# Mixer gates as 2x2 block products with seven multiplications, mixing in a fixed order, skip on ACT

## The chip, the cores and the metric

The kernel runs on one NeuronCore of a Trainium2 chip. The metric is device time in microseconds, from the start of the program on the chip to its end; lower is better. A core has a matmul engine (PE), a vector engine (DVE), a scalar engine for table functions (ACT), a general engine (POOL) and a queue that here only issues DMAs (SP). Each engine runs its own instructions in order; semaphores tie them together. All data is fp32.

## The reference

A small perceiver layer on x of 8 sequences x 64 tokens x 512 channels: cross attention to a long context, then a state space mixer, then a routed low-rank layer, each added to x. Only the mixer is touched. Per token, with 64 heads in 8 groups:

```
proj = hidden @ in_proj_w.T
gate = proj[..., :I];  hbc = proj[..., I:I + CONV_DIM];  dt = proj[..., -H:]
xBC  = silu(conv(hbc))                  # causal, 4 taps
y    = scan(xBC, softplus(dt), A) + x * D
y    = y / rms(y, per group) * norm_weight * silu(gate)
out  = y @ out_proj_w.T
```

## The kernel before

The mixer (`mixer_and_routed`) holds 512 tokens as four tiles of 128 (`tt`) and works group by group (`g` of 8). `xnT` is the normalized x, transposed: 4 blocks of 128 channels (`dc`) by 512 tokens. A group's input weights `G.w` are ten blocks of 128 output channels: four for the gates (n = 0 to 3), four for x (4 to 7), one each for B and C (8, 9).

- `project(G, n)`, L1101: four matmuls (one per `dc`) of 128x128 by 512 tokens into one PSUM bank of tag "pj", of which there are three. For a gate ACT applies SiLU to the bank (L1111, tile `sg`). For the others DVE runs the four taps (L1116, three times L1122, tile `acc`) and ACT the SiLU (L1127, tile `xbc`).
- `skip`, L1129: y = xbc times D, on POOL (L1134). `load_out`, L995: loads `w_out` and multiplies it by the norm's weight, on POOL (L1004).
- `steps` (POOL, tile `av`, four buffers) and `decay` (PE into two "seg" banks, L1093; ACT Exp, L1098) give a group's decay factors `dec`.
- `mix(G, tt)`, L1136: `pg` (PE), `gm` and `m` (DVE), `px` (PE transposes, L1154), `dx` (DVE). `scan(G, tt)`, L1165: 16 small matmuls `py`, then two DVE adds into `y` (L1178). `gate`, L1191: squares on ACT and POOL, and y times `sg` on DVE (L1194).
- `norm`, L1196: PE sums `pss` (L1200), ACT Ln and Exp (L1203, L1204). `project_out(G, tt)`, L1210: four matmuls into a bank of "pj", then DVE adds to x (L1217).

The groups are pipelined. In one round of the loop (L1275) group G is projected, the old group G-1 is mixed, scanned and gated between those projections, the decays of the new group G+1 follow, then the norm of the old one, then the four gates of G in turn with the four output projections of the old group. ACT needs one table for SiLU and another for Ln and Exp, so its work is kept in blocks by `tc.issue_after(ins)`: every instruction traced in such a block on the engine of `ins` is placed behind `ins` in that engine's queue (order only, no wait for it to finish). Beyond this a planner fixes each engine's order before the run: of the instructions that its own model of time takes to be ready, the one traced earliest goes first, and a tile's buffer is handed out when its first user is placed. The attention's projections already use block products with seven multiplications, by these two tables (L38):

```
FIRST = (("a", "L11", "R11"), ("d", "S2", "T2"), ("b", "S1", "T1"), ("c", "S3", "T3"))
SECOND = (("a", "L12", "R21"), ("b", "S4", "R22"), ("c", "L22", "T4"))
```

L are weight blocks, R token blocks, S sums of weight blocks (`weight_sums`, L137, four POOL adds), T differences of token blocks. The sums a and b lie in one PSUM bank, c and d in another. In the query stage (L209 to L235) `first` of a pair of heads is followed by `second` of the pair before, so one pair's sums are read while another's are computed.

Of the kernel before, what the change touches and what calls it, by code (L numbers as in the profile page):

```python
# [9 lines left out]
F32 = mybir.dt.float32  # L10
# [5 lines left out]
P = 128  # L16
# [934 lines left out]
def mixer_and_routed(ctx, tc, c, x, done, w_in, w_out, w_ra, b_w, out):  # L951
# [43 lines left out]
    def load_out(G):  # L995

        g = G.g
        G.wo = wst.tile([P, GC, D], F32, tag="w_out", name=f"w_out_{g}")
        nc.sync.dma_start(
            out=G.wo, in_=w_out[g * GC * P : (g + 1) * GC * P, :].rearrange("(n p) o -> p n o", p=P)  # L1000
        )
        for n in range(GC):
            ct = g * GC + n
            nc.gpsimd.tensor_scalar(G.wo[:, n, :], G.wo[:, n, :], c.nw[:, ct : ct + 1], None, op0=ALU.mult)  # L1004

    load_in(groups[0])

# [2 lines left out]
    for tt in range(NTT):  # L1010
# [9 lines left out]
            )  # L1020

    dt = big.tile([P, NTT, H2], F32, name="dt")
    z = big.tile([P, NTT, H2], F32, name="sp_z")
    nc.vector.tensor_tensor(z, pdt, c.dtb.unsqueeze(1).to_broadcast([P, NTT, H2]), ALU.add)
    e = big.tile([P, NTT, H2], F32, name="sp_e")

    nc.vector.tensor_scalar(dt, z, 0.0, None, op0=ALU.max)
    nc.vector.scalar_tensor_tensor(out=e, in0=dt, scalar=-2.0, in1=z, op0=ALU.mult, op1=ALU.add)
    nc.scalar.activation(e, e, AF.Exp)
    u = big.tile([P, NTT, H2], F32, name="sp_u")  # L1030
    nc.vector.tensor_scalar(u, e, 1.0, None, op0=ALU.add)
    lu = big.tile([P, NTT, H2], F32, name="sp_lu")
    nc.scalar.activation(lu, u, AF.Ln)
    nc.vector.tensor_scalar(u, u, 1.0, None, op0=ALU.subtract)
    nc.vector.tensor_scalar(z, u, 0.0, None, op0=ALU.is_equal)
# [10 lines left out]
        out=a, in0=dt, scalar=-1.0, in1=a_sb.unsqueeze(1).to_broadcast([P, NTT, H2]),  # L1046
        op0=ALU.mult, op1=ALU.mult,
    )

# [22 lines left out]
    def steps(G, tt):  # L1072


        if tt == 0:
            G.av, G.dec = [], grpp.tile([P, NTT, HPG, S], F32, tag="dec", name="dec")
        av = wk.tile([P, 2, HH, S], F32, tag="av", name="av", bufs=4)
        nc.gpsimd.tensor_tensor(
            av,
            ah[:, :, tt, G.g, :].unsqueeze(3).to_broadcast([P, 2, HH, S]),  # L1080
            c.upto1.unsqueeze(1).unsqueeze(1).to_broadcast([P, 2, HH, S]),
            ALU.mult,
        )
        G.av.append(av)
# [16 lines left out]
    def project(G, n):  # L1101

        pj = bank("pj", [P, NT], "pj", 3)
        for dc in range(DC):
            nc.tensor.matmul(  # L1105
                pj, lhsT=G.w[:, dc, n, :], rhs=xnT[:, dc, :], start=dc == 0, stop=dc == DC - 1
            )
        if n < GC:
            if n == 0:
                G.sg = grpp.tile([P, GC, NT], F32, tag="sg", name="sg")  # L1110
            return nc.scalar.activation(G.sg[:, n, :], pj, AF.Silu).ins  # L1111
        if n == 8:
            G.xbc = grpp.tile([P, GC + 2, NT], F32, tag="xbc", name="xbc")
        ct = G.g * GC + n - GC if n < 8 else (I2 // P + G.g if n == 8 else I2 // P + G2 + G.g)
        acc = wk.tile([P, NT], F32, tag="acc", name="acc", bufs=3)
        nc.vector.tensor_scalar(  # L1116
            acc, pj, c.cw[:, ct, KC - 1 : KC], c.cb[:, ct : ct + 1], op0=ALU.mult, op1=ALU.add
        )
        accb = acc.rearrange("p (b t) -> p b t", b=B)
        pjb = pj.rearrange("p (b t) -> p b t", b=B)  # L1120
        for k in range(1, KC):
            nc.vector.scalar_tensor_tensor(  # L1122
                out=accb[:, :, k:], in0=pjb[:, :, : S - k],
                scalar=c.cw[:, ct, KC - 1 - k : KC - k], in1=accb[:, :, k:],
                op0=ALU.mult, op1=ALU.add,
            )
        return nc.scalar.activation(G.xbc[:, n - GC, :], acc, AF.Silu).ins  # L1127

    def skip(G):  # L1129

        G.y = grpp.tile([P, GC, NT], F32, tag="y", name="y")
        for n in range(GC):
            ct = G.g * GC + n
            nc.gpsimd.tensor_scalar(G.y[:, n, :], G.xbc[:, n, :], c.dk[:, ct : ct + 1], None, op0=ALU.mult)  # L1134

    def mix(G, tt):  # L1136

# [72 lines left out]
    def project_out(G, tt):  # L1210
        po = bank("pj", [P, D], "mo", 3)
        for n in range(GC):
            nc.tensor.matmul(  # L1213
                po, lhsT=G.y[:, n, tt * P : (tt + 1) * P], rhs=G.wo[:, n, :],
                start=n == 0, stop=n == GC - 1,
            )
        nc.vector.scalar_tensor_tensor(  # L1217
            out=x[:, tt, :], in0=po, scalar=G.rs[tt], in1=x[:, tt, :], op0=ALU.mult, op1=ALU.add
        )


    w = big.tile([P, DC, E + E * R], F32, name="w_ra")
# [9 lines left out]
        nc.sync.dma_start(out=bw, in_=b_w)  # L1232

    def route(tt):
        xnT = wk.tile([P, DC, P], F32, tag="xnT", name="rt_xnT")
        layernorm_T(nc, c, small, ps, x, tt, xnT, tag="px", bufs=2, pbufs=1, copy=nc.scalar.copy)
        ph = bank("seg", [P, E + E * R], "ph", 2)
        for dc in range(DC):
            nc.tensor.matmul(
                ph, lhsT=xnT[:, dc, :], rhs=w[:, dc, :], start=dc == 0, stop=dc == DC - 1  # L1240
            )
        top = small.tile([P, 1], F32, tag="top", name="top")
        nc.vector.tensor_reduce(top, ph[:, :E], axis=AX.X, op=ALU.max)
        rw = small.tile([P, E], F32, tag="rw", name="rw")
        nc.vector.scalar_tensor_tensor(
            out=rw, in0=ph[:, :E], scalar=top, in1=rank, op0=ALU.is_equal, op1=ALU.mult
        )
# [12 lines left out]
        whT = wk.tile([P, P], F32, tag="whT", name="whT")  # L1260
        nc.scalar.copy(whT, pt)
        po = bank("y1", [P, D], "ro")
        nc.tensor.matmul(po, lhsT=whT, rhs=bw, start=True, stop=True)
        o = wk.tile([P, D], F32, tag="o", name="o")
        nc.vector.tensor_tensor(o, x[:, tt, :], po, ALU.add)
        nc.sync.dma_start(out=out[tt * P : (tt + 1) * P, :], in_=o)

# [1 line left out]
    g0 = groups[0]  # L1269
    for tt in range(NTT):  # L1270
        steps(g0, tt)
    last = None
    for tt in range(NTT):
        last = decay(g0, tt)
    for g in range(G2):  # L1275
# [10 lines left out]
        with tc.issue_after(last):  # L1286

            for n, behind in (
                (None, ((mix, 0),)),
                (8, ((mix, 1),)),  # L1290
                (9, ((scan, 0),)),
                (4, ((mix, 2), (scan, 1))),
                (5, ((gate, 0), (mix, 3), (scan, 2))),
                (6, ((gate, 1), (scan, 3))),
                (7, ((gate, 2), (gate, 3))),
            ):
                if n is not None:
                    silus.append(project(G, n))
                if old:
                    for what, tt in behind:  # L1300
                        what(old, tt)
            skip(G)
        with tc.issue_after(silus[-1]):
            table = load_ln_exp(nc).ins
        with tc.issue_after(table):
            if new:
                decay(new, 0)
                decay(new, 1)
        gates = [lambda n=n: project(G, n) for n in range(GC)]
        if new:  # L1310
            with tc.issue_after(table):
                last2 = decay(new, 2)
# [1 line left out]
        if old:  # L1314
            with tc.issue_after(table):
                last = norm(old, range(NTT))
        with tc.issue_after(last):
            for n in range(GC):
                if not new and n == NTT - 1:
                    scan(G, n)  # L1320
                    squares(G, n)
                last_gate = gates[n]()
                if not new:

                    for tt in ((0, 1), (2,), (3,), ())[n]:
                        mix(G, tt)
                    if 0 < n < NTT - 1:
                        scan(G, n - 1)
                        squares(G, n - 1)
                    if n == 2:  # L1330
                        scan(G, n)
                        squares(G, n)
                if old:
                    project_out(old, n)
        last = last_gate

    G = groups[-1]
# [77 lines left out]
```

## Time and profile before

| what | us |
|---|---|
| median of 3 runs | 2827.65 (2827.54 to 2829.23) |
| profiled execution, its own time | 2826.02 |
| span of its instructions | 2824.3 |
| one steady period of the mixer, 2400.35 to 2459.73 | 59.38 |
| PE busy in that period | 59.17 |
| DVE busy in that period | 31.13 |
| ACT, POOL busy in that period | 14.25, 23.20 |

The mixer's matmuls run from about 2324 us to the end; attention is before that. In the page's rows a group of instructions is named by line, engine, operation and tiles; a row of the timeline has start, duration, engine, line, operation, tiles, count and, in brackets, how long the engine stood idle before and what ended that. "seg", "pj" and "mo" are PSUM tiles; "mo" is the output projection and shares the "pj" banks. A few groups of the mixer (the columns after the count are busy us and mean ns of one, then idle before it):

```profile
L1105 PE MATMUL pj<-mx_xnT,w_in 128*128 128x512 f32 x640 | 296.3, 603 | 1.3 <-DVE acc L1122 1.3
L1134 POOL TENSOR_SCALAR y<-xbc,small_consts 128x512 f32<-128x512 f32 x32 | 55.7, 1740 | 50.1 <-ACT xbc L1127 50.1
L1004 POOL TENSOR_SCALAR w_out<-w_out,small_consts 128x512 f32<-128x512 f32 x32 | 49.6, 1567 | 179.3 <-DMA w_out<-in_w_out 176.7 <-DMA spare<-in_wo 2.6
L1111 ACT ACTIVATE sg<-pj 128x512 f32<-128x512 f32 x32 | 18.2, 596 | 86.9 <-PE pj L1105 86.8
```

A matmul's duration includes its passage through the pipeline, so the pace of PE is read from the starts. One projection (four matmuls) appears as eight records, 640 in all for 8 groups of 10 blocks.

### The profile page before, as it was taken

The numbers are of one execution on the slowest core, as the hardware profiler recorded it, in microseconds if no ns is written. First come the engines' busy times: TensorE is split into PE (matmuls) and PEld (weight loads), VectorE is DVE, ScalarE is ACT, GpSimd is POOL, SyncE is SP. The second block draws the span as 40 slices with busy tenths as digits, with TensorE's granted clock in tenths as the row PEclk, the third lists the DMA queues.
The fourth block names the chain that finished last, engine by engine and source line by source line (L and its number), as shares of the span: only waits on it lengthen the run. The fifth ranks groups of instructions, "written<-read, shape, count | busy, mean of one in ns | idle before, by whom it ended". The sixth has DMA issues, their size and how long they took to land.

```text
span 2824.3 us, 38454 instructions
## 1 busy us (share of the span) xinstructions
PE 2788.6 (99%) x14972; PEld 1980.9 (70%) x14972; DVE 1745.4 (62%) x3059; ACT 726.6 (26%) x1314; POOL 833.9 (30%) x786
## 2 busy tenths in 40 slices
PE   9899999999999999999999999999999999999998
PEld 7677777777777777777777777777777554444444
DVE  4556676676667666665666676667665416444555
ACT  3322223222222222232222222222222103222222
POOL 4323223222222332223222222322232223433431
PEclk9999999999999999999999999999999999999999
DMA  4822232232113122312311131122212441112200
GB/s 164 276 78 57 76 74 53 53 94 53 46 46 97 46 54 79 74 48 58 94 50 50 46 95 47 46 83 76 48 46 72 146 160 38 53 53 78 79 16 15
DMA packets 277230, 206.02 MB, mean 73 GB/s; under 512 B 155676, under 2 KB 240538, under 8 KB 276026
## 3 DMA queue, kind: packets, MB, share of 16 engines
q1 hardware_dynamic: 277050, 203.57, 25.2%
q8 instruction: 119, 1.95, 0.3%
q14 instruction: 61, 0.50, 0.1%
HBM read 180.87 MB, written 22.66 MB: 72 GB/s over the span
## 4 chain that ended last, share of the span: by engine, by line
PE 83%; DVE 6%; DMA 2%; ACT 1%; issue 0%; POOL 0%; SPq 0%; ACTq 0%; DVEq 0%
PE pav L596 12%; PE psc L526 11%; PE pj L1105 8%; PE pv_a L445 6%; PE pv_b L445 6%; PE pv_c L445 5%; PE pk_a L385 5%; PE pk_b L385 5%; PE pk_c L385 5%; PE mo L1213 4%; PE pv_d L445 3%; PE pk_d L385 2%; PE psn L414 2%; DMA nbs<-max_d 2%; DVE attn L574 1%; PE pvl L468 1%
## 5 line engine op out<-in xcount | busy, mean ns | idle before, releaser
L531 DVE SCALAR_TENSOR_TENSOR attn<-psc,rk,mask_sb 128x256 f32<-128x256 f32 (+1 forms) x832 | 363.4, 473 | 190.5 <-PE psc L526 188.1
L580 POOL TENSOR_TENSOR sm<-attn 128x512 f32<-128x512 f32 x64 | 82.0, 1281 | 1147.6 <-ACT attn L578 1147.6
L596 PE MATMUL pav<-attn,v 128*128 128x256 f32 (+1 forms) x1664 | 384.3, 381 | 0.0
L526 PE MATMUL psc<-q,kT 128*128 128x256 f32 x1536 | 371.5, 381 | 0.0
L596 PEld LDWEIGHTS pav<-attn,v 128*128 128x128 f32 (+1 forms) x1664 | 311.1, 190 | 55.4 <-issue 9.6
L583 POOL TENSOR_TENSOR sm<-sm,attn 128x512 f32<-128x512 f32 x256 | 339.8, 1328 | 29.4 <-DVE attn L574 10.6
L526 PEld LDWEIGHTS psc<-q,kT 128*128 128x128 f32 x1536 | 286.3, 190 | 82.4 <-issue 36.0
L1105 PE MATMUL pj<-mx_xnT,w_in 128*128 128x512 f32 x640 | 296.3, 603 | 1.3 <-DVE acc L1122 1.3
L574 DVE TENSOR_TENSOR attn<-attn,nb 128x1024 f32<-128x1024 f32 x192 | 224.7, 1216 | 68.2 <-ACT nb L571 67.9
L445 PEld LDWEIGHTS pv_a<-wv,cx 128*128 128x128 f32 x1536 | 195.5, 191 | 48.2 <-issue 41.4
L578 ACT ACTIVATE attn<-attn 128x1024 f32<-128x1024 f32 x192 | 202.5, 1058 | 71.3 <-DVE attn L574 68.5
L445 PE MATMUL pv_a<-wv,cx 128*128 128x128 f32 x1536 | 212.7, 279 | 0.0
L542 DVE TENSOR_TENSOR mx<-mx,attn 128x512 f32<-128x512 f32 x256 | 209.5, 818 | 2.0
L1105 PEld LDWEIGHTS pj<-mx_xnT,w_in 128*128 128x128 f32 x640 | 115.2, 190 | 129.4 <-issue 124.7
L385 PE MATMUL pk_a<-cx,wk 128*128 128x417 f32 (+1 forms) x512 | 193.3, 500 | 0.8 <-ACT qrs L110 0.8
L396 ACT ACTIVATE ksq<-kT 128x834 f32<-128x834 f32 (+1 forms) x128 | 109.0, 871 | 159.1 <-DVE kT L377 159.1
L637 POOL TENSOR_TENSOR o<-o,f 128x512 f32<-128x512 f32 x31 | 39.4, 1272 | 306.7 <-DMA f<-sums_d 206.3
L385 PEld LDWEIGHTS pk_a<-cx,wk 128*128 128x128 f32 x512 | 97.2, 190 | 46.1 <-issue 20.8
L1217 DVE SCALAR_TENSOR_TENSOR x<-mo,rs,x 128x512 f32<-128x512 f32 x32 | 24.0, 751 | 165.1 <-PE mo L1213 110.4
L1213 PE MATMUL mo<-w_out,y 128*128 128x512 f32 x256 | 118.1, 597 | 0.0
L571 ACT COPY nb<-nbs 128x256 f32<-128x256 f32 x64 | 24.1, 376 | 324.4 <-DMA nbs<-max_d 324.4
L1122 DVE SCALAR_TENSOR_TENSOR acc<-pj,small_consts,acc 128x504 f32<-128x504 f32 (+1 forms) x144 | 103.9, 725 | 0.7
(220 smaller groups left out, 4230.8 us busy)
## 6 DMA issues: line engine op xcount, KB each, us to landing
wk<-in_wk SPq DMA_DIRECT2D x32, 512.0 KB
wv<-in_wv SPq DMA_DIRECT2D x32, 512.0 KB
w_in<-in_w_in SPq DMA_DIRECT2D x16, 1024.0 KB
wvs<-wv_s_d SPq DMA_DIRECT2D x28, 512.0 KB
wks<-wk_s_d SPq DMA_DIRECT2D x28, 512.0 KB
cx<-in_ctxT SPq DMA_DIRECT2D x16, 834.0 KB
cx<-in_ctxT SPq DMA_DIRECT2D x16, 768.0 KB
wq<-in_wq SPq DMA_DIRECT2D x16, 512.0 KB
```

The costliest lines, as they stand in the source:

```text
L385: nc.tensor.matmul(ps[:, :w], lhsT=u.wk[l][:, dc, :], rhs=u.cx.r[ch][r][:, dc, :], start=start and dc == 0, stop=dc == 1, skip_group_check ...
L396: nc.scalar.activation(sq[ch][:, :, half, :w], u.kT[:, :, half, lo:hi], AF.Square)
L445: nc.tensor.matmul(ps[:, i * HD : (i + 1) * HD], lhsT=u.cx.r[ch][r][:, dc, i * P : (i + 1) * P], rhs=u.wv[l][:, dc, :], start=start and i ...
L526: nc.tensor.matmul(ps[:rows, t - t2, :], lhsT=lhsT, rhs=qh, start=True, stop=True)
L531: nc.vector.scalar_tensor_tensor(out=s.at[:rows, t, :].rearrange("p (h q) -> p h q", h=GQ), in0=ps[:rows, t - t2, :].rearrange("p (h q) -> ...
L542: nc.vector.tensor_tensor(s.mx2, s.mx2, s.at[:, t2 : t2 + 2, :], ALU.max)
L574: nc.vector.tensor_tensor(at[:, k : k + 4, :], at[:, k : k + 4, :], nb.unsqueeze(1).to_broadcast([P, 4, 256]), ALU.add,)
L578: nc.scalar.activation(at[:, k : k + 4, :], at[:, k : k + 4, :], AF.Exp)
L583: nc.gpsimd.tensor_tensor(sm2, sm2, at[:, i : i + 2, :], ALU.add)
L596: nc.tensor.matmul(s.av[:, 0, :], lhsT=u.v[:rows, t, hh, :], rhs=s.at[:rows, t, :], start=t == 0, stop=t == NKT - 1,)
L1105: nc.tensor.matmul(pj, lhsT=G.w[:, dc, n, :], rhs=xnT[:, dc, :], start=dc == 0, stop=dc == DC - 1)
L1213: nc.tensor.matmul(po, lhsT=G.y[:, n, tt * P : (tt + 1) * P], rhs=G.wo[:, n, :], start=n == 0, stop=n == GC - 1,)
```

## The change

The four gate blocks of a group become two 2x2 block products over two halves of the channels and two halves of the tokens (256 each), with seven multiplications each, into two "pj" banks. Token differences are made once, weight sums per group. `skip` and the weighing of `w_out` go from POOL to ACT. Mix and scan are placed on PE behind the projection that they follow in the list, and in the gates' stage the order on PE is fixed: first, second, two output projections, first, second, two output projections. To make room in SBUF some tiles share buffers.

```diff
-        for n in range(GC):
-            ct = g * GC + n
-            nc.gpsimd.tensor_scalar(G.wo[:, n, :], G.wo[:, n, :], c.nw[:, ct : ct + 1], None, op0=ALU.mult)
+    def weigh_out(G):
         for n in range(GC):
+            ct = G.g * GC + n
+            nc.scalar.activation(G.wo[:, n, :], G.wo[:, n, :], AF.Copy, scale=c.nw[:, ct : ct + 1])
+    def sums_in(G, n):
+        l = {
+            f"L{k + 1}{e + 1}": G.w[:, 2 * e : 2 * e + 2, n + k, :] for k in range(2) for e in range(2)
+        }
+        G.l = getattr(G, "l", {})
+        G.l[n] = weight_sums(nc, l, wk.tile([P, 4, 2, P], F32, tag="ws", name="ws"))
...
+    sp = grpp.tile([P, GC, NT], F32, tag="y", name="sp")
...
+    ts = big.tile([P, 4, 2, HT], F32, name="mx_xs")
+    blocks.update((f"T{k + 1}", ts[:, k]) for k in range(4))
+    def token_sums():
+        for o, p, q in (
+            ("T1", "R12", "R11"), ("T2", "R22", "T1"), ("T3", "R22", "R12"), ("T4", "R21", "T2")
+        ):
+            nc.vector.tensor_tensor(blocks[o], blocks[p], blocks[q], ALU.subtract)
...
-        av = wk.tile([P, 2, HH, S], F32, tag="av", name="av", bufs=4)
+        av = wk.tile([P, 2, HH, S], F32, tag="av", name="av", bufs=3)
...
+    def project_gates(G, n):
+        st, l = Group(), G.l[n]
...
+        def first():
+            st.ps = {}
+            for pair in ("ab", "cd"):
+                t = bank("pj", [P, 2, HT], f"pj_{pair}", 3)
+                st.ps[pair[0]], st.ps[pair[1]] = t[:, 0, :], t[:, 1, :]
+            for k, lhs, rhs in FIRST:
+                last = product(k, lhs, rhs, k in "ad", False)
+            p1 = wk.tile([P, HT], F32, tag="p1", name="p1", bufs=1)
+            nc.scalar.copy(p1, st.ps["a"])
+            st.u2 = wk.tile([P, HT], F32, tag="u2", name="u2", bufs=1)
+            nc.vector.tensor_tensor(st.u2, p1, st.ps["d"], ALU.add)
+            nc.vector.tensor_tensor(p1, st.u2, st.ps["b"], ALU.add)
+            nc.vector.tensor_tensor(to[:, 1, HT:], p1, st.ps["c"], ALU.add)
+            return last
+        def second():
+            for k, lhs, rhs in SECOND:
+                last = product(k, lhs, rhs, False, True)
+            nc.scalar.activation(to[:, 0, :HT], st.ps["a"], AF.Silu)
+            nc.vector.tensor_tensor(to[:, 0, HT:], st.u2, st.ps["b"], ALU.add)
+            nc.vector.tensor_tensor(to[:, 1, :HT], st.u2, st.ps["c"], ALU.add)
+            nc.scalar.activation(to[:, 0, HT:], to[:, 0, HT:], AF.Silu)
+            return last, nc.scalar.activation(to[:, 1, :], to[:, 1, :], AF.Silu).ins
...
-            nc.gpsimd.tensor_scalar(G.y[:, n, :], G.xbc[:, n, :], c.dk[:, ct : ct + 1], None, op0=ALU.mult)
+            nc.scalar.activation(G.y[:, n, :], G.xbc[:, n, :], AF.Copy, scale=c.dk[:, ct : ct + 1])
...
-                    silus.append(project(G, n))
+                    done, silu = project(G, n)
+                    silus.append(silu)
                 if old:
-                    for what, tt in behind:
-                        what(old, tt)
+                    with tc.issue_after(done if n is not None else done_out):
+                        for what, tt in behind:
+                            what(old, tt)
             skip(G)
+        if g == 0:
+            token_sums()
+            sums_in(G, 0)
+            sums_in(G, 2)
...
         with tc.issue_after(last):
-            for n in range(GC):
...
+            for k in range(2):
+                first, second = project_gates(G, 2 * k)
+                if k:
+                    own((scan, 3), (squares, 3))
+                    with tc.issue_after(done_out):
+                        done_in = first()
+                else:
+                    done_in = first()
+                    own((mix, 0), (mix, 1))
+                with tc.issue_after(done_in):
+                    done_out, last_gate = second()
+                if not k:
+                    own((scan, 0), (squares, 0))
+                for tt in (2 * k, 2 * k + 1):
+                    if old:
+                        with tc.issue_after(done_out):
+                            done_out = project_out(old, tt)
+                    if not k:
+                        own((mix, tt + 2), (scan, tt + 1), (squares, tt + 1))
+                if new:
+                    sums_in(new, 2 * k)
+            weigh_out(G)
```

`own` runs its steps on G itself in the last round only, where there is no new group. The routed tail takes its `xnT` from the buffers of `sq` and its output tile from those of `acc`.

More of the change, by code (lines that the diff above doesn't have):

```diff
@@ L1022, in mixer_and_routed @@
     dt = big.tile([P, NTT, H2], F32, name="dt")
-    z = big.tile([P, NTT, H2], F32, name="sp_z")
+    sp = grpp.tile([P, GC, NT], F32, tag="y", name="sp")
+    z, e, u, lu = (
+        sp[:, k, : NTT * H2].rearrange("p (t h) -> p t h", h=H2) for k in range(4)
+    )
     nc.vector.tensor_tensor(z, pdt, c.dtb.unsqueeze(1).to_broadcast([P, NTT, H2]), ALU.add)
-    e = big.tile([P, NTT, H2], F32, name="sp_e")
     nc.vector.tensor_scalar(dt, z, 0.0, None, op0=ALU.max)
@@ L1029, in mixer_and_routed @@
     nc.scalar.activation(e, e, AF.Exp)
-    u = big.tile([P, NTT, H2], F32, name="sp_u")
     nc.vector.tensor_scalar(u, e, 1.0, None, op0=ALU.add)
-    lu = big.tile([P, NTT, H2], F32, name="sp_lu")
     nc.scalar.activation(lu, u, AF.Ln)
@@ L1048, in mixer_and_routed @@
     )
+    HT = NT // 2
+    blocks = {
+        f"R{e + 1}{half + 1}": xnT[:, 2 * e : 2 * e + 2, half * HT : (half + 1) * HT]
+        for e in range(2) for half in range(2)
+    }
+    ts = big.tile([P, 4, 2, HT], F32, name="mx_xs")
[5 more added lines that the diff above has]
+            nc.vector.tensor_tensor(blocks[o], blocks[p], blocks[q], ALU.subtract)
     psw = bank("seg", [P, NTT, H2], "psw", 2)
@@ L1104, in project @@
         for dc in range(DC):
-            nc.tensor.matmul(
+            done = nc.tensor.matmul(
                 pj, lhsT=G.w[:, dc, n, :], rhs=xnT[:, dc, :], start=dc == 0, stop=dc == DC - 1
[L1107 to L1111, printed above, removed]
+            ).ins
         if n == 8:
@@ L1126, in project, with product @@
             )
-        return nc.scalar.activation(G.xbc[:, n - GC, :], acc, AF.Silu).ins
+        return done, nc.scalar.activation(G.xbc[:, n - GC, :], acc, AF.Silu).ins
+    def project_gates(G, n):
+        st, l = Group(), G.l[n]
+        if n == 0:
+            G.sg = grpp.tile([P, GC, NT], F32, tag="sg", name="sg")
+        to = G.sg[:, n : n + 2]
+        def product(k, lhs, rhs, start, stop):
+            for dc in range(2):
+                last = nc.tensor.matmul(
+                    st.ps[k], lhsT=l[lhs][:, dc, :], rhs=blocks[rhs][:, dc, :],
+                    start=start and dc == 0, stop=stop and dc == 1, skip_group_check=True,
+                ).ins
+            return last
[12 more added lines that the diff above has]
+            nc.vector.tensor_tensor(to[:, 1, HT:], p1, st.ps["c"], ALU.add)
+            return last
+        def second():
[6 more added lines that the diff above has]
+            return last, nc.scalar.activation(to[:, 1, :], to[:, 1, :], AF.Silu).ins
+        return first, second
     def skip(G):
@@ L1212, in project_out @@
         for n in range(GC):
-            nc.tensor.matmul(
+            last = nc.tensor.matmul(
                 po, lhsT=G.y[:, n, tt * P : (tt + 1) * P], rhs=G.wo[:, n, :],
@@ L1219, in project_out @@
         )
+        return last.ins
     w = big.tile([P, DC, E + E * R], F32, name="w_ra")
@@ L1234, in route @@
     def route(tt):
-        xnT = wk.tile([P, DC, P], F32, tag="xnT", name="rt_xnT")
+        xnT = wk.tile([P, DC, P], F32, tag="sq", name="rt_xnT")
         layernorm_T(nc, c, small, ps, x, tt, xnT, tag="px", bufs=2, pbufs=1, copy=nc.scalar.copy)
@@ L1263, in route @@
         nc.tensor.matmul(po, lhsT=whT, rhs=bw, start=True, stop=True)
-        o = wk.tile([P, D], F32, tag="o", name="o")
+        o = wk.tile([P, D], F32, tag="acc", name="o", bufs=3)
         nc.vector.tensor_tensor(o, x[:, tt, :], po, ALU.add)
@@ L1271, in mixer_and_routed @@
         steps(g0, tt)
-    last = None
+    last = done_out = None
     for tt in range(NTT):
@@ L1308, in mixer_and_routed @@
                 decay(new, 1)
-        gates = [lambda n=n: project(G, n) for n in range(GC)]
         if new:
@@ L1316, in mixer_and_routed, with own @@
                 last = norm(old, range(NTT))
+        def own(*what):
+            if not new:
+                for step, tt in what:
+                    step(G, tt)
         with tc.issue_after(last):
-            for n in range(GC):
[L1319 to L1334, printed above, removed]
+            for k in range(2):
[20 more added lines that the diff above has]
+            weigh_out(G)
         last = last_gate
```

## The prediction

> **What bounds the kernel now.** I read the page's busy times first, then the chain of waits, then the mixer stage alone, because the change touches nothing before 2300 us.
>
> ```profile
> span 2824.3 us, 38454 instructions
> PE 2788.6 (99%) x14972; PEld 1980.9 (70%) x14972; DVE 1745.4 (62%) x3059; ACT 726.6 (26%) x1314; POOL 833.9 (30%) x786
> PE 83%; DVE 6%; DMA 2%; ACT 1%; issue 0%; POOL 0%; SPq 0%; ACTq 0%; DVEq 0%
> ```
>
> PE is the bound: 99% busy, 83% of the chain. The mixer repeats every 59.4 us: the product of y and the gate that the chain passes starts at 2400.35, 2459.73, 2518.99, 2578.39. One period, cut where its character changes, by a view of busy time per stretch:
>
> ```profile
> core 0: us, PE busy (x) PEld busy (x) DVE busy (x) ACT busy (x) POOL busy (x), PEclk, DMA share, GB/s
> 2431.46:2463.40 31.94, 31.94 (x227) 15.37 (x227) 28.88 (x49) 5.67 (x9) 18.50 (x16) 1.00 0.28 96
> 2463.40:2472.40 9.00, 8.79 (x46) 3.86 (x45) 0.00 (x0) 5.02 (x12) 4.69 (x4) 1.00 0.01 2
> 2472.40:2490.90 18.50, 18.50 (x47) 7.93 (x46) 2.27 (x4) 3.56 (x5) 0.00 (x0) 1.00 0.12 36
> ```
>
> Stretch A (first row) runs from the first mix of the old group to the end of the last convolution: DVE has 28.88 of 31.94 us, so it is nearly a bound itself. B (second row) is a chain on ACT. C (third row) is PE alone: gates and output projections. PE is full in all three, in B only because there is unrelated work for it:
>
> ```profile
> 2463.40 0.63 ACT L1127 ACTIVATE xbc<-acc 128x512 f32<-128x512 f32 x1 [3.73 <-DVE acc L1122]
> 2464.05 1.28 ACT L116 ACT_TABLE_LOAD   x1
> 2465.34 0.66 ACT L1098 ACTIVATE dec<-seg 128x256 f32<-128x256 f32 x2
> 2466.75 0.66 ACT L1098 ACTIVATE dec<-seg 128x256 f32<-128x256 f32 x2 [0.75 <-PE seg L1093]
> ...
> 2470.06 0.66 ACT L1098 ACTIVATE dec<-seg 128x256 f32<-128x256 f32 x2 [0.99 <-PE seg L1093]
> 2471.89 0.26 ACT L1203 ACTIVATE rs<-pss,eps 128x4 f32<-128x4 f32 x1 [1.17 <-PE pss L1200]
> 2472.18 0.20 ACT L1204 ACTIVATE rs<-rs 128x4 f32<-128x4 f32 x1
> 2472.40 1.28 ACT L1111 ACT_TABLE_LOAD   x1
> ```
>
> Last SiLU, table load, four decays that alternate with PE, the norm's Ln and Exp. Project 7 ends on PE at 2458.6 (its start 2455.16 plus 3.43). From there to the Exp's end are 13.8 us, in which PE's own share of the chain is four seg blocks of 0.6 and pss 0.95, about 3.4 us. The other 10.3 us are filled by exactly three projections of 3.43 us: gate 0, output projection 0 and gate 1. Three is the number of "pj" banks.
>
> **Part 1: fewer multiplications.** The pace of eight 128x512 matmuls, from the chain in order of time, and of 128x256 ones, from the query stage, where the same seven products run:
>
> ```profile
> 2417.73 3.43 PE pj L1105 x8
> 2421.16 3.43 PE mo L1213 x8
> ```
>
> ```profile
> 103.64 1.03 PE L204 MATMUL pq_cd<-xs,wqs 128*128 128x256 f32 x4
> 103.84 0.37 ACT L220 COPY q_p<-pq_ab 128x256 f32<-128x256 f32 x1 [1.02 <-PE pq_ab L204]
> ...
> 104.50 1.03 PE L204 MATMUL pq_ab<-xnT,wq 128*128 128x256 f32 x4
> 104.77 0.42 DVE L222 TENSOR_TENSOR q_u<-q_p,pq_cd 128x256 f32<-128x256 f32 x1 [3.10 <-PE pq_cd L204]
> ...
> 105.23 0.42 DVE L224 TENSOR_TENSOR q_t<-q_u,pq_ab 128x256 f32<-128x256 f32 x1
> ```
>
> 3.43/8 = 0.429 us against (104.50-103.64)/4 = 0.215 us. Each fp32 matmul is two instructions here (a projection's 4 are 8 records). Gates before: 4x8x0.429 = 13.73 us a group. After: two block products of 7x2x2 = 28 records, 56x0.2155 = 12.07. Gain 1.66 us a group, 13.3 in eight. The Trainium skill speaks against this: "TensorE: Matmul & The Clock Gate", section Back-to-back issue gap, gives sustained 131 ns at 512 columns and 81 ns at 128, so about 98 at 256 by my interpolation; 56x98 = 5.5 us against 32x131 = 4.2 would make the blocks 1.3 times dearer (+4 us a group on our 13.73). The trace halves cleanly at 256 columns, so the row decides.
>
> **Part 2: the new wait, the crux.** The second half of a block product accumulates onto banks that the first half's evacuation must have read. Two things delay that. (a) p1 is an ACT copy traced behind `last`, the norm's Exp: it cannot issue before the end of B. (b) Sums a and b share a bank, so do c and d. The query rows show what this does: the copy of a starts at 103.84, after b's matmuls have ended, although a ended 1.7 us earlier; u2 waits for c; and the read of b ends at 105.65, 1.15 us after the last matmul of the first half issued out (104.50). There another pair's second half fills the hole; here second follows first directly. So `second` of pair 0 starts after Exp + copy 0.4 + u2 0.5 + sum 0.5 = 1.4 us more, and `second` of pair 1 has a hole of 1.25 us. And the output projections, which may go between in the old code, now stand behind `second` (issue_after(done_out)): of the three fillers of B one is left, `first` of pair 0, 3.45 us. PE would lack 6.9 us there.
>
> **What can fill it.** Mixing of the next round is barred too. Projections 8 and 9 of the next group carry no edge on PE; w_in has landed (DMA burst at 2431-2445). Does this program's order reach across groups? It did once:
>
> ```profile
> 2353.97 0.33 PE L1154 MATMUL px<-ident,xbc 128*128 128x128 f32 x1
> 2355.59 0.70 PE L1105 MATMUL pj<-mx_xnT,w_in 128*128 128x512 f32 x1 [1.29 <-DVE acc L1122]
> ```
>
> That transpose belongs to the next round and stands before group 0's gates. So I take it that project 8 (3.43), then mix 1 behind it (0.9), go into B on the third bank, and project 9 starts once that bank's convolution (0.81 + 3x0.73 = 3.0 us) is done.
>
> **Part 3: off POOL, onto ACT and DVE.** POOL loses 4x1.74 (skip) and 4x1.57 (w_out) and gains 8 weight sums at 0.78 (the query rows L141 to L144, 0.75 to 0.82) = 6.2 us; it has slack either way. ACT gains 8 copies of 128x512 at 0.63 (row L1127) and about 1 us in the gates. Only skip 3 matters: it is ready with the last SiLU and traced before the table load, +0.63 us in B; if ordered behind, 0. Should Copy need a table, each change costs 1.28 us; the skill ("ScalarE: Activation LUTs", Table sets) says copy is in every set, which no row here shows. I take 0. DVE gains 10 adds of 0.42 a group in C, where it had 2.27 us of work in 18.5: hidden. Without POOL's skip beside them, gate products may fall from 0.89 to 0.68 us: 0 to -0.8 in A, kept for the range. The four token sums (1.2 us each in the query stage) fall once into DVE's idle 6.4 us before 2350.78; uncovered they cost 4.7. av with three buffers waits for seg 0, 3 segs ahead of its use: 0. Shared tiles in the softplus and the routed tail: used once, at times far apart: 0, at worst 1 us. load_in's DMAs are let go earlier (w_in is done before the last two output projections): 0. The fixed order of mix and scan is the order that PE already shows between 2431 and 2455: 0.
>
> **Sum for a steady group.** A: DVE 28.88 - two convolutions 6.0 = 22.9, plus some 2.1 of its 3.1 us idle = 25.0 (PE needs 23.7 there: mixing and scan 5.9, four projections 13.7, seg, `first`). B: 9.0 + 0.63 + 1.4 = 11.1. C: second 2.6, two outputs 6.87, first 3.45, hole 1.25, second 2.6, two outputs 6.87, two bank waits of 0.3 = 24.2. Total 60.3 against 59.4: +0.95, in six groups +5.7. Group 0: its gates end later by what projections 8 and 9 are earlier, 0. Group 7: no decays, but nothing of a next group either; after 3.45 of `first` and 1.7 of mixing PE waits about 3.0 us, scan 0 and mix 2 fill 1.6; +1.4 +1.25 +0.6 -1.66 = about +1.5. Together +7.2. The profiled execution's own time is 2826.02 (span 2824.3 and 1.7 around it), 1.6 below the median; put on the median 2827.65 this gives **2835 us**.
>
> **Rivals.** *Fully filled* (the other side): fillers cover all PE idle, leaving the gain of part 1: 2827.65 - 13.3 = 2814 at best. For: PE's content of a period is only 57.7 us, and A+B+C could be as short with DVE at 0.68 a product. Against: one bank serves projections 8 and 9 in turn, with 3 us of convolution between. It decides where PE's added idle stays under 1.66 us a group. *Nothing fills*: A stays about 31, B shrinks to 9.8 as decays alternate faster, C 24.2: 65, +5.6 in six groups, +2 to +4 at each end: about 2866. For: one transpose is thin evidence. The same skill page (Part 1) lets an idle window of 3.4 us halve the clock; this trace shows granted 1.00 through the mixer, and segs split the holes, so I add nothing; if it fell, about 2 us a group more. *Fill, but misplaced*: fillers fixed in an order that the chip's times don't match, PE stuck behind a bank: +2.5 to +4.5 a group, 2843 to 2855. That the change doesn't do what it says is out: the matmul count is fixed by the code.
>
> **Chances.** A measurement tells 0.2%, 5.7 us, from nothing. Forecast (2824 to 2845) 45%: slower 27, same 16, faster 2. Fully filled 25%: faster 22, same 3. Nothing fills 18% and misplaced 12%: slower. So faster 0.24, same 0.19, slower 0.57. Range 2815 to 2862; the likeliest case's own is 2824 to 2845.
>
> **What would show it.** Right: gate records 128x256, starts 0.215 apart; p1's copy behind the norm's Exp; a projection of the next group inside B; a hole near 1.2 us before pair 1's second. Wrong: period under 59; output projections before second; Copy with a table load; PE idle above 5 us in B.

## The result: slower by 2.6%, and the profile after

The changed kernel takes 2901.53 us (median of 4 runs, 2900.43 to 2905.73) against 2827.94: ratio 1.0262, 95% interval 1.0244 to 1.028. Slower was the likelier sign of the prediction, but +74 us was far outside its range of 2815 to 2862. The page of the changed kernel, in the lines that answer to those of before:

```profile
span 2898.7 us, 39021 instructions
PE 2808.4 (97%) x15164; PEld 2039.9 (70%) x15164; DVE 1779.3 (61%) x3143; ACT 775.7 (27%) x1410; POOL 774.4 (27%) x786
PE 83%; DVE 5%; DMA 2%; ACT 1%; issue 1%; SPq 0%; ACTq 0%; DVEq 0%
```

PE has 20 us *more* busy time although it multiplies less, and is still "97% busy": matmuls at half clock last longer and count as busy. Neither the page's shares nor its chain by engine say where 74 us went. The stages do. One round, the first behind the start, cut at the last SiLU, the norm's Exp and close to the first mix; and, in the fourth row, stretch A of the next round, cut exactly at the first mix and the last SiLU:

```profile
core 0: us, PE busy (x) PEld busy (x) DVE busy (x) ACT busy (x) POOL busy (x), PEclk, DMA share, GB/s
2382.40:2413.73 31.33, 31.03 (x234) 16.40 (x232) 29.26 (x50) 9.06 (x16) 9.75 (x13) 1.00 0.26 84
2413.73:2424.74 11.01, 5.97 (x32) 3.43 (x32) 0.00 (x0) 5.62 (x14) 3.12 (x3) 0.59 0.00 0
2424.74:2451.80 27.06, 24.63 (x76) 14.92 (x76) 6.43 (x14) 7.12 (x14) 5.65 (x8) 0.91 0.22 75
2451.63:2483.54 31.91, 31.61 (x233) 16.43 (x232) 28.71 (x49) 7.62 (x13) 6.93 (x9) 1.00 0.17 55
```

Stretch A (first and fourth rows) did not shrink: it takes 31.9 us in every later round, as before, and still has some 233 PE records. B (second row) is 11 us with PE busy 5.97. In B and C the granted clock, the number after POOL's, is no longer 1.00. The timeline of ACT, PE and DVE through B:

```profile
2413.73 0.63 ACT L1149 ACTIVATE xbc<-acc 128x512 f32<-128x512 f32 x1 [3.15 <-DVE acc L1144]
2414.37 1.28 ACT L116 ACT_TABLE_LOAD   x1
2415.67 0.72 ACT L1200 ACTIVATE y<-xbc,small_consts 128x512 f32<-128x512 f32 x1
2416.30 0.64 ACT L1124 ACTIVATE dec<-seg 128x256 f32<-128x256 f32 x2
...
2416.71 1.40 PE L1119 MATMUL seg<-av,past 64*64 64x256 f32 x8 [3.28 <-ACT dec L1124]
...
2418.59 1.40 PE L1119 MATMUL seg<-av,past 64*64 64x256 f32 x8 [0.48 <-ACT dec L1124]
...
2422.34 1.86 PE L1266 MATMUL pss<-ones,s 128*128 128x1 f32 x8 [0.48 <-ACT dec L1124]
...
2424.54 0.20 ACT L1270 ACTIVATE rs<-rs 128x4 f32<-128x4 f32 x1
2424.65 0.35 ACT L1177 COPY p<-pj_ab 128x256 f32<-128x256 f32 x1
...
2425.03 0.42 DVE L1179 TENSOR_TENSOR u<-p,pj_cd 128x256 f32<-128x256 f32 x1 [11.34 <-ACT p L1177]
2425.49 0.42 DVE L1180 TENSOR_TENSOR p<-u,pj_ab 128x256 f32<-128x256 f32 x1
...
2426.05 2.04 PE L1162 MATMUL pj_ab<-mx_xnT,w_in 128*128 128x256 f32 x4 [1.85 <-DVE p L1180]
...
2437.27 1.03 PE L1162 MATMUL pj_ab<-mx_xnT,w_in 128*128 128x256 f32 x4
2438.14 1.03 PE L1162 MATMUL pj_cd<-mx_xs,ws 128*128 128x256 f32 x4
2439.00 1.03 PE L1162 MATMUL pj_ab<-mx_xs,ws 128*128 128x256 f32 x4
...
2442.00 1.10 PE L1162 MATMUL pj_ab<-mx_xnT,w_in 128*128 128x256 f32 x4 [1.11 <-DVE p L1180]
```

Read it upwards from the row at 2426.05; the four rows below that are pair 1. The second half of pair 0 (2426.05) waits for the read of bank ab, that for u, that for the copy of a, and the copy stands on ACT right behind the norm's Exp. Until then PE has only the decays and the norm's sums, and stands idle for 3.28, 0.48, 0.57, 0.48 and 1.85 us; pair 1 adds 1.11. That is **7.8 us idle per group**, where before it was 0.2. The list of PE's waits (us in total, times, longest) says the same in two lines; before, the first stood at 1.1 us and the second did not exist:

```profile
PE seg L1119 <- ACT dec L1124: 28.7, 21, 3.3
PE pj_ab L1162 <- DVE p L1180: 20.0, 14, 2.0
```

And a block of eight seg records takes 1.40 us where it took 0.66 at full clock. The period went from 59.2 to 69.8 us (means of five, by the starts of pss). Of the 74.4 us that the span grew, five periods hold 52.8, the time before the first pss 10.8 and that behind the sixth 10.8.

### The profile page after: what moved, and what is told of

Its sections match the earlier page's. It is cut to its first block, busy times and chain, and to the rows that moved or that the text cites. A ratio compares the mean times of both kernels' runs of the same rounds, so it can differ in the third digit from the quotient of the medians.

```text
span 2898.7 us, 39021 instructions
## 1 busy us (share of the span) xinstructions
PE 2808.4 (97%) x15164; PEld 2039.9 (70%) x15164; DVE 1779.3 (61%) x3143; ACT 775.7 (27%) x1410; POOL 774.4 (27%) x786
## 4 chain that ended last, share of the span: by engine, by line
PE 83%; DVE 5%; DMA 2%; ACT 1%; issue 1%; SPq 0%; ACTq 0%; DVEq 0%
PE pav L596 12%; PE psc L526 11%; PE pv_a L445 6%; PE pj L1131 6%; PE pv_b L445 5%; PE pv_c L445 5%; PE pk_a L385 5%; PE pk_b L385 5%; PE pk_c L385 5%; PE mo L1279 4%; PE pv_d L445 3%; PE pk_d L385 2%; PE pj_ab L1162 2%; DMA nbs<-max_d 2%; PE psn L414 2%; PE pj_cd L1162 1%
## 5 line engine op out<-in xcount | busy, mean ns | idle before, releaser
L583 POOL TENSOR_TENSOR sm<-sm,attn 128x512 f32<-128x512 f32 x256 | 339.7, 1327 | 29.4 <-DVE attn L574 10.6
L1131 PE MATMUL pj<-mx_xnT,w_in 128*128 128x512 f32 x384 | 176.3, 601 | 0.0
L1131 PEld LDWEIGHTS pj<-mx_xnT,w_in 128*128 128x128 f32 x384 | 69.1, 190 | 72.3 <-issue 70.3
L375 ACT COPY kT<-pk_a 128x384 f32<-128x384 f32 x64 | 31.5, 493 | 265.8 <-PE pk_a L385 265.8
```

What stands on the lines that cost most here:

```text
L583: nc.gpsimd.tensor_tensor(sm2, sm2, at[:, i : i + 2, :], ALU.add)
L1131: done = nc.tensor.matmul(pj, lhsT=G.w[:, dc, n, :], rhs=xnT[:, dc, :], start=dc == 0, stop=dc == DC - 1).ins
```

## Experiments

All are edits of the changed kernel; ratios are against the kernel before, on the same chip.

**Is it the gates at all?** `gates4` puts the four plain gate projections back and leaves everything else of the change.

```diff
-            for k in range(2):
-                first, second = project_gates(G, 2 * k)
...
+            for n in range(GC):
+                done_out, last_gate = project(G, n)
...
+                if old:
+                    done_out = project_out(old, n)
```

> The changed kernel with its four gate projections put back as four plain projections in turn with the output projections; skip and the weighing of w_out stay on ACT, mix and scan stay in the fixed order. My theory: the whole loss sits in the block products' place in the gates' stage, so this is within 0.3% of the kernel before, 2820 to 2834 us, with PE full between the decays and granted clock 1.00. Rival (the work moved to ACT or the fixed order lengthens the chain of SiLU, table and decays): 2850 us or more, with idle PE before the first seg.

2835.62 us, ratio 1.0022 (1.0013 to 1.0032): just above what was expected. The blocks and their placing cost some 66 us of the 74. The rest belongs to what `gates4` keeps (skip and weighing on ACT, the fixed order, the token sums and the shared buffers) together; these are taken apart only in part below.

**Is it the copy of a behind Exp?** `dve` moves that one copy from ACT to DVE; `early` leaves it on ACT but traces the first half of pair 0 ahead of the block that stands behind Exp. Both take away the same wait by different means, so that an effect of the engine can be told from one of the place in the queue.

```diff
# dve
-            nc.scalar.copy(p1, st.ps["a"])
+            nc.vector.tensor_copy(p1, st.ps["a"])
# early
+        first, second = project_gates(G, 0)
+        done_in = first()
         with tc.issue_after(last):
...
-                    done_in = first()
```

> The changed kernel with one edit: the copy of the sum a out of PSUM is made by DVE instead of ACT, so that it does not stand behind the norm's Exp in ACT's queue. My theory: second of the first pair then runs between the decays, and output projection 0 behind it, so that only the two waits of second for first's evacuation remain (about 1.8 and 1.1 us a group) against the gain of 1.66: 2832 to 2848 us, clock 1.00. Rival (it is the output projections' place behind second that costs, not the copy's place): 2870 us or more.

> The changed kernel with first of the first pair traced ahead of the block that is ordered behind the norm's Exp, so that ACT still copies sum a, but may do it before the norm. My theory: it is the copy's place in ACT's queue that made the hole, not the engine; the time is that of the copy on DVE within 6 us: 2833 to 2846 us. Rival (ACT is too busy with table load and decays to copy in time, so the engine matters): 2850 us or more.

2838.83 us (1.0037, 1.0025 to 1.0049) and 2837.94 (1.0032, 1.002 to 1.0044), both as expected. One instruction's place in ACT's queue is worth 63 us. Since `early` keeps the copy on ACT and is as fast, it is the place and not the engine. The second half can now run inside B, and behind it the output projections. The waits of PE in `dve`:

```profile
PE pj_ab L1162 <- DVE p L1180: 17.1, 14, 1.6
```

The wait for seg has gone from the list; the wait of the second half for its bank stays (in one group 1.63 us for pair 0 and 0.97 for pair 1).

**And the barrier of the output projections?** `free` only takes away the order that holds them behind the second half; `dve_free` does so on top of `dve`.

```diff
-                        with tc.issue_after(done_out):
-                            done_out = project_out(old, tt)
+                        done_out = project_out(old, tt)
```

> The changed kernel with the output projections free to stand before second; the copy of a stays behind the norm's Exp. My theory: one output projection (3.43 us) takes the third bank in the hole, and no second one can, because its bank is read only after the norm: about half of the idle time and most of the low clock go, 2855 to 2876 us. Rival (the order behind second was the whole cause): below 2840 us. Rival (it was none of it): above 2890 us.

> The copy of sum a made by DVE, and the output projections without the order behind second. My theory: two matmuls of an output projection then stand in each of the two holes between first and second, which were 1.63 and 0.97 us in the run with the copy on DVE alone; the steady period falls from 60.3 to 57.9 to 58.4 us, and the time to 2819 to 2829 us, at or below the kernel before. Rival (the holes come from the chain of the decays, so that the fillers only move): 2834 us or more.

`free`: 2857.58 us (1.0106, 1.009 to 1.0121). `dve_free`: 2824.89 (0.9986, 0.998 to 0.9993), period 58.2. Each edit alone leaves a wait, and the two together remove the loss: now pair 0's wait for the bank is covered by output projections, and pair 1's too. The sum of the single gains (62.7 + 44.0) is more than the gain of both (76.6), since they fill the same holes.

**Skip and weighing on ACT?** `dve_free_pool` puts both back on POOL.

```diff
-            nc.scalar.activation(G.y[:, n, :], G.xbc[:, n, :], AF.Copy, scale=c.dk[:, ct : ct + 1])
+            nc.gpsimd.tensor_scalar(G.y[:, n, :], G.xbc[:, n, :], c.dk[:, ct : ct + 1], None, op0=ALU.mult)
```

> As the run before it in this call, and skip and the weighing of w_out back on POOL. The run with plain gates had a period of 59.9 instead of 59.4 us, and PE stood idle 0.8 instead of 0.2 us before the second seg block. My theory: that is the last skip on ACT (0.72 us) between table load and first decay, and putting it back on POOL gives 0.3 to 0.6 us a group: 2 to 4 us below the run before it, 2815 to 2826 us. Rival (POOL's skips slow DVE beside them, which costs as much): no difference or slower.

2823.2 us (0.9983, 0.9976 to 0.9991): within the forecast, but its interval overlaps that of `dve_free`, so the gain of this part is not shown. The trace has the mechanism: the first Exp follows the table load directly here, where in the changed kernel 0.72 us of skip stand between. B of this kernel, rows of the timeline as above:

```profile
2408.24 1.28 ACT L116 ACT_TABLE_LOAD   x1
...
2409.43 0.59 PE L1162 MATMUL pj_ab<-mx_xnT,w_in 128*128 128x256 f32 x2
2409.53 0.66 ACT L1124 ACTIVATE dec<-seg 128x256 f32<-128x256 f32 x2
2410.06 0.84 PE L1119 MATMUL seg<-av,past 64*64 64x256 f32 x8
2410.83 0.70 PE L1162 MATMUL pj_ab<-mx_xnT,w_in 128*128 128x256 f32 x2
```

The second half of the block product now runs in pieces between the decays: the holes are filled with the group's own work, the first seg block takes 0.84 us as it did before, and no idle of PE stands in these rows.

**Why did nothing of the next group fill the holes?** `y0` gives project 8 a bank of another tag, which is idle in B.

```diff
-        pj = bank("pj", [P, NT], "pj", 3)
+        pj = bank("y0", [P, NT], "pj") if n == 8 else bank("pj", [P, NT], "pj", 3)
```

> The changed kernel with one edit: projection 8 takes its bank from the tag y0 instead of pj. My theory: in the changed kernel projection 8 of the next group could not move into the hole because the banks of one tag are handed out in traced order and the output projections come first; with a bank of another tag it stands there (3.43 us of the 3.3 us hole). Then the hole closes and the clock stays up through the seg blocks: 6.5 to 8 us a group less, 2848 to 2864 us. Rival (the hole is only moved, since projection 8 is taken from a stretch in which DVE was the bound anyway): 2870 to 2901 us.

2872.47 us (1.0153, 1.0139 to 1.0167). The fill that the prediction had assumed now takes place:

```profile
2416.55 2.74 PE L1131 MATMUL pj<-mx_xnT,w_in 128*128 128x512 f32 x6
2420.00 0.93 PE L1119 MATMUL seg<-av,past 64*64 64x256 f32 x8 [0.71 <-ACT dec L1124]
2420.86 1.13 PE L1131 MATMUL pj<-mx_xnT,w_in 128*128 128x512 f32 x2
```

So the bank kept it out. The reading that fits is that the third bank goes to the output projections, which are traced earlier and wait behind the second half; in `free`, where they don't wait, one of them runs in this very place. Stretch A of the next round falls from 31.9 to 28.5 us, by one projection. That speaks against the rival, which let DVE hold A, although the time lies in the rival's range. The gain (29 us) is short of the expected 37 to 54, because the clock still falls, only later. Three stretches of B and C of this run, in the columns of the first such table, and stretch A of the next round:

```profile
2411.80:2418.80 7.00, 7.00 (x32) 4.30 (x30) 5.11 (x7) 3.12 (x4) 2.27 (x3) 1.00 0.00 0
2418.80:2426.20 7.40, 4.96 (x36) 2.25 (x34) 3.01 (x4) 3.99 (x13) 3.13 (x3) 1.00 0.00 0
2426.20:2432.60 6.40, 5.22 (x12) 4.21 (x13) 1.26 (x3) 4.24 (x7) 1.39 (x3) 0.52 0.01 3
2454.16:2482.68 28.52, 28.52 (x227) 15.42 (x227) 26.17 (x45) 6.93 (x11) 6.91 (x9) 1.00 0.21 62
```

It is low for 6.8 us there, of which PE is idle for about 1.0; 5.8 us of work at half speed lose 2.9 us. In four of the six steady rounds it is low that long, in two for 3.4 us, which lose 1.7: about 15 us in all (an estimate from these figures), close to the 16 us by which the time lies above the middle of its bracket.

**What is the clock's own price?** Three runs put matmuls that nobody reads into the holes and leave the chain alone.

```diff
# warm: four of 128x512 between the halves of pair 0
+                        idle = bank("px", [P, NT], "idle")
+                        for _ in range(4):
+                            done_in = nc.tensor.matmul(
+                                idle, lhsT=c.ident, rhs=xnT[:, 0, :], start=True, stop=True
+                            ).ins
# warm2: one behind each decay, four behind pss, four and two between the halves
# warm3: of 128x256; seven behind decay 0, one behind each other decay, four behind pss, two in pair 1
```

> The changed kernel plus four matmuls of 512 columns per group whose result nobody reads, placed on PE between first and second of the first pair, where PE stands idle. They change no wait. My theory: the idle time of over 3 us lets the granted clock fall to half for the 8 to 9 us that follow, which costs 4.8 us a group on the seg blocks, pss and the first sums of second; with PE kept at work the clock stays at 1.00 and the time falls by about 30 us, to 2866 to 2880 us. Rival (the low clock has another cause, or the seg blocks are slow for another reason): 2897 to 2906 us, seg blocks still 1.3 to 1.4 us.

> The changed kernel with matmuls in every hole of the stretch behind the table load, read by nobody: one behind each of the four decay blocks, four behind the norm's sums and two between the first and the second half of pair 1 (10 per group, 128x512, about 0.43 us each). The chain that sets the end (table load, decay, norm's Exp, copy of p, second half) is left as it is. Theory, clock: with the holes closed the granted clock stays near 1.00 and the segment blocks, the norm's sums and the second half keep their usual durations; that returns most of the 4.8 us a group that half speed costs: 2862 to 2882 us. Rival, waits alone: half speed only stretches work in front of waits that end later anyway, so the time stays at 2890 to 2902 us although the clock is up.

> The changed kernel with unread matmuls of 128x256 that are sized to the holes: seven behind the first decay block's matmuls, one behind each of the other three, four behind the norm's sums, two between the halves of pair 1. A 128x256 matmul is two records of 0.215 us, so 14 of them are 6.0 us of the 7.8 us that TensorE stands idle per group, in places where it waited. (The run warm2 had 14 matmuls of 128x512, which are 28 records of 0.43 us, 12 us per group: it closed the holes and then overfilled them, and its clock stayed at 0.999.) Theory, clock and holes add up: the granted clock stays near 1.00 and the period falls from 70.1 to 65.3 us, by the 4.8 us that half speed cost; 2864 to 2876 us. Rival, waits alone: the period stays at 69.5 us or more, 2894 us or more.

`warm` missed: 2897.58 us (1.0242, 1.0228 to 1.0256). It closed the first hole, seg was quick again, but the holes of 0.71, 0.58, 0.48 and 1.85 us stayed and the clock fell at the last of them, so that the second half took 5.3 us from its start to the next matmul's, where it took 4.4 in the changed kernel and takes 2.7 at full clock (pair 1). `warm2` missed as well: 2911.58 us (1.0301, 1.0285 to 1.0317) at a clock of 0.999. Both its theories had mispriced the filler: a 128x512 matmul is two records of 0.43 us, and there are 14 a group, not 10; they are 12.0 us, and overfill. Its sum closes all the same: 69.8 - 4.8 (clock) - 7.1 (holes) + 12.0 = 69.9, measured period 70.25. `warm3`, sized to the holes, gives 2878.57 us (1.0177, 1.016 to 1.0194), 3 us above its bracket. It holds 16 fillers, not the 14 that its expectation counts, 6.9 us a group. Clock through B and into C:

```profile
2476.60:2483.60 7.00, 6.33 (x32) 5.24 (x28) 3.93 (x5) 3.79 (x7) 1.04 (x1) 1.00 0.00 0
2483.60:2489.20 5.60, 5.58 (x41) 3.36 (x42) 0.00 (x0) 2.23 (x8) 3.13 (x3) 1.00 0.01 3
2489.20:2493.80 4.60, 4.58 (x21) 3.74 (x21) 1.27 (x3) 4.54 (x9) 0.74 (x2) 1.00 0.00 0
```

Useless work makes the kernel 23 us faster, and the period 66.2 us, 3.6 shorter. That is a lower bound on the clock's price, since the fillers may themselves delay a little; the lengthened blocks of the changed kernel's first round (seg three times about +0.7, pss +0.9, second half +1.8) add up to 4.8. So the clock is at least a third of the 10.6 us that the period grew, and by the longer figure just under half.

**Token sums.** `best_tok` is `dve_free_pool` with the four sums placed later on DVE, behind its copy into `ah` (`on_dve`).

```diff
-            token_sums()
+            with tc.issue_after(on_dve):
+                token_sums()
```

> The kernel with the copy of p on VectorE, the output projections freed and skip and weighing on GpSimd, with the four token sums placed behind VectorE's copy into ah, so no longer inside the softplus chain at the start. Theory: the first decay block moves up by 1.5 to 2 us, and PE's hole of 3.3 us at the first group's start shrinks: 2820.5 to 2822.5 us against 2823.2 us. Rival: PE has projections to do there anyway and the hole moves: 2823 us, no difference.

2819.56 us (0.9973, 0.9964 to 0.9982), 1 us below its bracket, against 2823.2 (0.9983, 0.9976 to 0.9991): the intervals overlap, so the last step of time is not shown by these. The trace shows the mechanism: from the last pdt to the first seg 14.74 us, where it was 16.46 in the changed kernel and in `dve_free_pool`, and 14.75 before; and PE's hole ahead of the first gates is 1.54 us instead of 3.26. As a whole this version is faster than the kernel before by 0.27% (0.18 to 0.36), about 8 us.

## Why the prediction was right and wrong

**Right.** The pace of 256 columns: the first half of pair 1 has four records each from 2437.27, 2438.14 and 2439.00 on, 0.216 us a record; so the rows decided rightly, and not the 98 ns that Part 1 had interpolated. The size of the hole: Part 2 said that PE would lack 6.9 us in B, and the five holes there add up to 6.7. The wait itself: p1's copy behind Exp, and the second half 1.31 us after Exp's end (1.4 said), 1.11 us of hole in pair 1 (1.25 said). Copy needs no table: the loads are as many as before. The fixed order of mix and scan costs nothing that shows in the steady rounds: A is 31.9 us, as before. The three runs `dve`, `early` and `free` show that this wait and the barrier are the cause, as Part 2 had it.

**Wrong, the step that failed: "What can fill it".** It let project 8, a mix and project 9 move into B and so took A down from 31.9 to 25.0. One transpose, standing before a gate, was generalized to projections, which need a "pj" bank, and no bank came free for them ahead of the barred output projections. Measured (B and C in the round from 2413.73, A in the round behind it; over the next five rounds B is 11.5 to 12.3 and C 25.4 to 26.8):

| stretch | predicted | nothing fills (rival) | measured |
|---|---|---|---|
| A, first mix to last SiLU | 25.0 | 31 | 31.9 |
| B, to pair 0's second half | 11.1 | 9.8 | 12.3 |
| C, to the next first mix | 24.2 | 24.2 | 25.6 |
| sum | 60.3 | 65 | 69.8 |

A alone is 6.9 of the 9.5 us that the sum was short. The rival, given 18%, had A right, and B and C but for the clock: in `warm3`, at full clock, A, B and C are 31.9, 10.4 and 23.9, 66.2 in all. Its 2866 us already lay outside the range of 2815 to 2862. `y0` shows the bank to be the reason, and that giving project 8 another one moves this projection alone.

**Wrong, a cost put at nothing: the clock.** The rival's 65 and the measured 69.8 differ by 4.8 us, in B and C mostly, where the clock was low. The prediction held that rule and row disagreed: the page of the Trainium skill "TensorE: Matmul & The Clock Gate" (Part 1) lets an idle window of some 3.4 us halve the clock, the trace of before had 1.00 throughout the mixer, and "segs split the holes". But PE had no hole above 1.3 us in the mixer before, so that 1.00 was no evidence on this. The query stage of the same trace had one of 2.27 us (86.84 is its end), and there the clock did fall, from 1.00 in the first row to 0.50 in the second (columns as in the tables of stretches):

```profile
84.57:87.99 3.42, 1.16 (x6) 1.05 (x6) 0.00 (x0) 0.75 (x1) 3.00 (x6) 1.00 0.92 273
87.99:91.40 3.41, 3.41 (x9) 2.71 (x9) 0.05 (x1) 0.37 (x1) 2.75 (x4) 0.50 0.96 326
```

It was sized at 2 us a group "if it fell"; it fell and cost 3.6 to 4.8. In the round shown the first hole of 3.28 us was enough, and the clock was halved 2.4 us into it.

**Wrong, a cost put at nothing: the token sums.** "They fall once into DVE's idle 6.4 us". They were placed between the steps of the softplus instead, each step of which the first seg waits for:

```profile
2329.94 0.42 DVE L1038 TENSOR_TENSOR sp<-pdt,small_consts 128x256 f32<-128x256 f32 x1 [0.41 <-PE pdt L1027]
2330.28 0.68 DVE L1074 TENSOR_TENSOR mx_xs<-mx_xnT,mx_xs 128x512 f32<-128x512 f32 x1
2330.88 0.29 DVE L1040 TENSOR_SCALAR dt<-sp 128x256 f32<-128x256 f32 x1
2331.08 0.68 DVE L1074 TENSOR_TENSOR mx_xs<-mx_xnT 128x512 f32<-128x512 f32 x1
```

They delay it by 1.71 us (16.46 against 14.75), and a hole of 3.26 us opens in group 0 where it was 1.29. "Uncovered they cost 4.7" was too dear by the other side: 0.68 us each, not 1.2.

**Sizes.** The three projections that filled B before don't fit it exactly, as was read: gate 1 ends at 2473.51, 1.1 us behind the Exp's end. Skip 3 stands behind the table load, not ahead of it, but delays decay 0 just as was said, by 0.72 us instead of 0.63. Of the gain of 1.66 us a group 1.0 to 1.1 are seen once the waits are gone: the period is then 58.1 to 58.2 us. The two ends were put at 0 and +1.5 us and measure 10.8 each. Of the first, 1.06 lies ahead of the mixer, where nothing was changed; behind that, group 0 has the holes of the steady rounds too, 8.0 us of idle PE where it was 1.3. The last end was not taken apart, and its cause stays open.

## What to carry to other kernels

An edit that takes multiplications away is worth what its new dependences leave of it: before adding a copy or a sum that frees a PSUM bank, look at what stands ahead of it in that engine's queue, and which matmuls stand behind the one that waits for the bank. Don't count on later work to move into a hole unless its PSUM bank is free of others that stand in line for it. And price PE's idle time twice: as the hole, and, where a trace of the same kernel shows the clock fall behind a hole of that size, as the half clock on what comes after it.

## What the runs showed of the hardware

The granted clock falls to exactly 0.50 and can stay there after PE is busy again. The changed kernel in steps of 3.41 us, laid so that one ends at the fall (2415.82) and one at the rise (2429.47):

```profile
2412.41:2415.82 3.41, 1.02 (x5) 0.57 (x3) 1.25 (x2) 2.06 (x3) 0.00 (x0) 1.00 0.00 0
2415.82:2419.23 3.41, 2.04 (x13) 1.14 (x16) 0.00 (x0) 1.77 (x5) 0.99 (x1) 0.50 0.00 0
2419.23:2422.65 3.42, 2.38 (x18) 0.82 (x10) 0.00 (x0) 1.32 (x4) 1.69 (x3) 0.50 0.00 0
2422.65:2426.06 3.41, 1.56 (x9) 1.50 (x8) 0.96 (x3) 1.79 (x5) 0.45 (x1) 0.50 0.00 0
2426.06:2429.47 3.41, 3.41 (x8) 2.78 (x9) 0.30 (x1) 2.68 (x4) 0.00 (x0) 0.50 0.02 5
2429.47:2432.88 3.41, 3.41 (x11) 1.94 (x11) 0.75 (x2) 1.32 (x3) 2.82 (x4) 1.00 0.00 0
```

It fell 2.4 us into the hole and rose 13.7 us later, 3.4 us after PE's last hole. In each of the thirteen traces of this case all changes of the granted clock stand whole steps of 3.41 us apart, and the low stretches that end within a trace last one to four steps (3.4, 6.8, 10.2 or 13.7 us). This agrees with Part 1 of the same page of the Trainium skill, which gives 3.41 us for a free-running window. In these traces a low step was followed by full clock whenever PE was busy for 2.76 us of it or more, and never where it was busy for 2.61 or less. That is why the clock stays low all through B of the changed kernel, whose holes leave no step full before the second half runs, and why in `y0` and `warm`, where it falls only in B's last hole, it is back after one or two steps.

The fall is less sharp. No step has to be idle throughout: PE had worked 1.0 us of the one ahead of the fall in the changed kernel, 1.9 in `y0` and at most 2.5 in any trace. Every step at full clock with less than 1.4 us of work was followed by a fall, but of those with 1.4 to 2.5 us some were and some were not. So the two holes a group of `dve`, 0.97 and 1.63 us, which leave about 1.8 us of work in the emptiest step, left the clock at 1.00 through the whole period from 2405 to 2465. What decides between these, the runs don't settle.
